# Expert blocks in pairs: 256 moving tokens, gating by chunks, the short rests of two blocks in the row halves of TensorE

## The chip, the cores and the metric

The kernel runs on one core of a Trainium2 chip. The metric is device time in microseconds (us) of one execution; lower is better. All arithmetic is in float32 but for the aggregation of the second layer.

## What is computed

Two layers on 2708 rows of 256 channels, with a 2708 x 2708 adjacency matrix. Each layer is a graph attention step and then a mixture of experts (MoE), each with a residual; layer 0 has an ordinary causal attention ahead of its MoE. Cut to what matters here, the MoE of both layers is:

```python
logits = flat @ router_w.T
topk_probs, topk_idx = top_k(softmax(logits), 2)
gates = ...                      # two of eight experts per row, normalised
for e in range(8):               # w1, w3: 682 x 256, w2: 256 x 682
    hh = silu(flat @ w1[e].T) * (flat @ w3[e].T)
    out = out + gates[:, e:e + 1] * (hh @ w2[e].T)
```

and a layer is

```python
x = x + gnn(layernorm(x), adj)
x = x + ffn(layernorm(x))
```

Layer 1's graph step normalises and projects the rows of layer 0's result (x1 in the kernel), and aggregates them with a masked softmax over the adjacency.

## The kernel before, in words

The rows are cut into 22 tiles of 128. The program runs in four stages: the first layer up to its routing, the experts of layer 0 (experts_blocks with layer 0), the second layer's graph step up to its routing, and the experts of layer 1. A fallback branch at the end is not taken with this input.

**The two list-scheduled stages.** The first and the third stage are lists of steps. Class Plan (L70) holds for each step its engine, an estimated length, what it needs, the buffers that it takes and gives, a rank, and `lands`, the time that is expected to pass from a DMA's issue to its landing. Plan.issue goes through the list with these estimates and writes out the instructions of each engine in the resulting order; so the estimates decide which instruction stands ahead of which in an engine's queue, and the real waits decide when it runs. Gaps that the plan expects on TensorE are filled with matmuls that nobody reads (L1666).

**Places of the experts.** Routing sends each row, by an indirect DMA (L1805), to a place in the buffer xs of the expert that it goes to. Every expert has six blocks of 128 places (NB = 6). Some blocks are not run by experts_blocks but as steps of the lists, by some_blocks: the EARLY ones of layer 0 and of layer 1 (three and four blocks) at the end of the first and third stage, and the two LATE ones of layer 0, (7, 4) and (7, 5), at the head of the third stage. That leaves 43 blocks for experts_blocks in layer 0 and 44 in layer 1. The late blocks are in lines L533 (transposes), L540 (copies on ACT), L555 (up), L561 to L565 (memset and Silu), L570 to L572 (multiplications on DVE), L578 (down), L582 (weighing) and add_rows.

**One block.** The rows of a block are fetched from xs into a tile xt by SP (L2000), transposed on TensorE with the identity (L278) and copied to SBUF by ACT (L280, or L283 with a scale in layer 0): that is front. Then up (L2017) runs 22 matmuls with 128 moving columns: the hidden width of 682 is five chunks of 128 and a rest of 42 (NF = 5, REST = 42), each chunk for w1 and for w3 with two halves of the 256 channels; the rests of w1 and w3 share one weight tile, w3's columns at 0 and w1's at 64 (HIGH). All go to one tile of three PSUM banks, of which there are two. ACT then takes the Silu of all five chunks in one instruction (L2021), DVE multiplies in one (L2022), and both do the rest of 42 rows (L2024, L2025), giving hT. Then down (L2031) runs six matmuls with hT's chunks as weights and 256 columns of w2 as moving data, into y; the sixth chunk is the rest, filled with zeros to 128 rows. DVE weighs y with the gate (L2033), and GpSimd adds the rows to the result in HBM with an indirect accumulating DMA (add_rows, L611). These adds go to the same array, so each waits for the one before it to have landed.

**The order in experts_blocks.** It is written out by hand: in iteration k come the fetch of block k+3, at one place of every expert the load of the weights of expert e+2 into the one of three rooms that e-1 had (load_expert, L1966 to L1978, DMAs on SP, memsets on GpSimd), then up(k), front(k+2), and down(k-1). Tests of the routing's counts on TensorE and DVE stand ahead of block (2, 0). At the end comes the down of the last block.

**The head of the third stage.** x1, the result of layer 0 in HBM, is loaded by SP in five pieces (L1514 to L1517). The first three, up to tile 12, need the adds of experts_blocks to have landed; the last two need the late blocks' adds too. prepare (L1450 on) makes of each tile of x1 the normalised and projected rows: statistics on DVE, a power on GpSimd (L1458), scaling on DVE (L1462), transposes and matmuls on TensorE (L1477), copies on ACT. Masks come from HBM by transposing DMAs (L1541, L1545). Aggregation computes the attention weights (L1556 on ACT, L1565 and L1571 on DVE) and multiplies on TensorE (L1578, into po).

**Memory.** experts_blocks opens pools of its own (bkeep for hT and one room of weights, slot for xt, xT, sl and ys); the third stage's list has its own work tiles. When a pool is closed, the next one takes the same memory, and an instruction that writes there first waits for what last read it.

Of the kernel before, what the change touches and what calls it, by code (L numbers as in the profile page):

```python
# [20 lines left out]
P = 128  # L21
# [124 lines left out]
def adj_ffn_kernel(ctx, tc, x, adj, vecs, bias_rows, tab, w_gnn0, w_gnn1, wqkv, wo,  # L146
# [1263 lines left out]
    def second(X, XB, xs0, x1, x2, sd, mb, xs, arena, load_weights):  # L1410
# [9 lines left out]
        with ExitStack() as s:  # L1420
# [93 lines left out]
            for a, b in zip((0,) + ends, ends):  # L1514
                loads.append(add("SP", 0.45 * (b - a), lambda a=a, b=b: nc.sync.dma_start(
                    out=X[:, a:b, :], in_=x1[a * P:b * P, :].rearrange("(t p) c -> p t c", p=P)),
                    late, rank=-9.0, lands=2.0 if 0 < a < LATE_T else 14.0 if a == 0 else 7.0))  # L1517
                if b == LATE_T:
                    late = some_blocks(add, 0, [(*b, []) for b in LATE], [XR[:, k, :] for k in range(len(LATE))], [],
                                       lambda e: weights_at(arena[:, WE:]), xs0, x1, new, named, -20.0)  # L1520
                    for e in late:
                        e["needs"] += loads
# [289 lines left out]
    def after_all(i, xs):  # L1812
        for name in written[xs.name]:
            tc.add_manual_dep(i.ins, name, NEEDS, reason="reads what they wrote")
# [152 lines left out]
    def load_expert(room, w1, w3, w2, e):  # L1967
        cut = NF * P
        a, b, c, d = weights_at(room)
        nc.gpsimd.memset(c, 0.0)  # L1970
        nc.gpsimd.memset(d[:, NF, :], 0.0)
        w1v, w3v = (w[:, e, :].rearrange("(k p) h -> p k h", p=P) for w in (w1, w3))
        nc.sync.dma_start(out=a, in_=w1v[:, :, :cut])
        nc.sync.dma_start(out=b, in_=w3v[:, :, :cut])
        nc.sync.dma_start(out=c[:, :, :REST], in_=w3v[:, :, cut:])
        nc.sync.dma_start(out=c[:, :, HIGH:], in_=w1v[:, :, cut:])
        nc.sync.dma_start(out=d[:, :NF, :], in_=w2[e, :cut, :].rearrange("(k p) c -> p k c", p=P))
        nc.sync.dma_start(out=d[:REST, NF, :], in_=w2[e, cut:, :])  # L1978

    def experts_blocks(layer, w1, w3, w2, xs, acc, arena):  # L1980

# [3 lines left out]

        with ExitStack() as s:
            keep = s.enter_context(tc.tile_pool(name=f"bkeep{layer}", bufs=1))
            hTs = [keep.tile([P, NHC, P], F32, name=f"hT{i}") for i in range(3)]
            for hT in hTs:
                nc.gpsimd.memset(hT[:, NF, :], 0.0)  # L1990
            rooms = [arena[:, :WE], arena[:, WE:], keep.tile([P, WE], F32, name="room")]

            with tc.tile_pool(name=f"slot{layer}", bufs=2) as sp, \
                    tc.tile_pool(name=f"bpu{layer}", bufs=2, space=PSUM) as pu, \
                    tc.tile_pool(name=f"bpt{layer}", bufs=1, space=PSUM) as pt_:

                def fetch(e, j):
                    xt = sp.tile([P, ROW], F32, tag="xt", name="xt", bufs=5)
                    row = e * CAP + j * P
                    after_all(nc.sync.dma_start(out=xt, in_=xs[row:row + P, :]), xs)  # L2000
                    return xt

                def front(xt):
                    xT = sp.tile([P, KC, P], F32, tag="xT", name="xTs", bufs=3)
                    transpose_row(xT, xt, P, pt_, V_LN2 if layer == 0 else None)
                    return xT

                def up(k, w, xT):

                    pp = pu.tile([P, 3 * GW // P, P], F32, tag="pp", name="pup")  # L2010
                    for n in range(2 * NF + 1):
                        if n < 2 * NF:
                            wn, to = w[n // NF][:, :, n % NF * P:(n % NF + 1) * P], P
                        else:
                            wn, to = w[2], HIGH + REST
                        for c in range(KC):
                            nc.tensor.matmul(pp[:to, n, :], wn[:, c, :], xT[:, c, :],  # L2017
                                             start=(c == 0), stop=(c == KC - 1))
                    hT = hTs[k % len(hTs)]
                    sl = sp.tile([P, NF, P], F32, tag="sl", name="sl")  # L2020
                    nc.scalar.activation(sl, pp[:, :NF, :], AF.Silu)  # L2021
                    nc.vector.tensor_tensor(hT[:, :NF, :], sl, pp[:, NF:2 * NF, :], ALU.mult)  # L2022
                    sr = sp.tile([P, P], F32, tag="sr", name="sr")
                    nc.scalar.activation(sr[:REST], pp[HIGH:HIGH + REST, 2 * NF, :], AF.Silu)  # L2024
                    nc.vector.tensor_tensor(hT[:REST, NF, :], sr[:REST], pp[:REST, 2 * NF, :], ALU.mult)  # L2025
                    return hT

                def down(e, w, hT, xt):
                    y = pt_.tile([P, C], F32, tag="y", name="y")
                    for n in range(NHC):  # L2030
                        nc.tensor.matmul(y, hT[:, n, :], w[3][:, n, :], start=(n == 0), stop=(n == NHC - 1))  # L2031
                    ys = sp.tile([P, C], F32, tag="ys", name="ys", bufs=3)
                    nc.vector.tensor_scalar(ys, y, xt[:, C + 1 + e:C + 2 + e], None, ALU.mult)  # L2033
                    add_rows(layer, acc, ys, xt)

                done = [b[:2] for b in EARLY[layer]] + list(() if layer else LATE)
                blocks = [(e, j) for e in range(NE) for j in range(NB) if (e, j) not in done]
                xt = [fetch(*blocks[k]) for k in range(3)]
                nxt = [front(xt[k]) for k in range(2)]
                last = None  # L2040
                for k, (e, j) in enumerate(blocks):
                    if k + 3 < len(blocks):
                        xt.append(fetch(*blocks[k + 3]))
                    if j == (2 if e else 3) and e + 2 < NE:
                        load_expert(rooms[(e + 2) % 3], w1, w3, w2, e + 2)
                    if (e, j) == (2, 0):

                        pc = pt_.tile([P, C], F32, tag="y", name="pc")
                        nc.tensor.matmul(pc[:, :NE], allones, hsum[:, NT, :], start=True, stop=True)
                        nc.vector.tensor_tensor(counts[:, layer, :], pc[:, :NE], part, ALU.subtract)  # L2050

# [3 lines left out]
                        for i, (e_, t, places, test) in enumerate(tests):  # L2055
# [1 line left out]
                            nc.tensor.matmul(pc[:, at:at + 1], allones, hsum[:, t, e_:e_ + 1], start=True, stop=True)  # L2057
                            to = i + layer * (FLAGS - len(EARLY[1]))
                            nc.vector.tensor_scalar(missed[:, to:to + 1], pc[:, at:at + 1], float(e_ * CAP + places), None, test)
                    if layer == 1 and (e, j) == (3, 0):  # L2060
                        raise_flag(keep, lambda name: pt_.tile([P, C], F32, tag="y", name=name))
                    xT = nxt[k]
                    we = weights_at(rooms[e % 3])
                    hT = up(k, we, xT)
                    if k + 2 < len(blocks):
                        nxt.append(front(xt[k + 2]))
                    if last is not None:
                        down(*last)
# [151 lines left out]
```

## Time and profile before

| | us |
|---|---|
| three runs | 1554.26, 1555.1, 1552.09 (median 1554.26) |
| the profiled execution, whole | 1553.19 |
| its span in the profile | 1551.5 |
| TensorE busy | 1468.3 |
| DVE / ACT / GpSimd busy | 740.9 / 551.9 / 533.0 |
| mean granted TensorE clock | 0.982 of full |

The lines of the profile are read so: a line of a group has the source line, the engine, the operation, output <- inputs, the tile of the PE array that it uses (rows*columns), its shape, how many there are, and after the bar the busy time, the mean in ns of one, and the idle time of the engine just before them with what ended it. A line of the timeline has start, length, engine, source line and operation, how many instructions it sums up, and in brackets the idle time before it and what ended that. SPq is the DMA queue that SP feeds. A float32 matmul shows as two records of the PE. Records overlap in time, because matmuls are pipelined, so what one costs is read from start to start.

The four stages in this execution: the experts of layer 0 run to about 845 us, the second layer's graph step to about 1193 us, the experts of layer 1 from there to the end.

### The profile page before, as it was taken

How to read it: one execution, taken by the hardware profiler on the slowest of the kernel's cores; microseconds unless marked ns; L12 is line 12 of the kernel's file. 1: busy time of each engine (PE TensorE's matmuls, PEld its weight loads, DVE VectorE, ACT ScalarE, POOL GpSimd, SP SyncE). 2: the span in 40 equal slices, each digit the busy share in tenths (PEclk: the TensorE clock that was granted, in tenths of full speed). 3: DMA queues.
4: the chain of work that ended last, by engine and by line, in shares of the span. 5: the costliest groups of instructions: out<-in, count | busy, mean ns of one | idle time of the engine just before them, and what ended most of it. 6: DMA issues, size and time to landing. Idle time of an engine off the chain costs nothing. (4 is left out here: it accounts for less than half of the span.)

```text
span 1551.5 us, 23359 instructions
## 1 busy us (share of the span) xinstructions
PE 1468.3 (95%) x8988; PEld 1153.4 (74%) x8988; DVE 740.9 (48%) x1450; ACT 551.9 (36%) x1068; POOL 533.0 (34%) x695
## 2 busy tenths in 40 slices
PE   6878899999999999999999899999999999999995
PEld 5633433433437899999999678888778999999995
DVE  6688999966685122222221554867753222222221
ACT  3577766754544111111111453443332111111110
POOL 6677679681163222222222300030444222222221
PEclk9899999999999999999999999999999999999998
DMA  7689767620013332333222850541414333332211
GB/s 261 214 274 316 238 231 252 193 67 8 7 54 94 96 75 53 90 90 90 36 36 33 177 117 1 132 111 61 149 58 109 79 87 88 74 87 50 34 34 17
DMA packets 168029, 165.68 MB, mean 107 GB/s; under 512 B 81384, under 2 KB 148264, under 8 KB 165200
## 3 DMA queue, kind: packets, MB, share of 16 engines
q1 hardware_dynamic: 142582, 134.26, 28.5%
q0 software_dynamic: 21056, 26.24, 9.9%
q10 hardware_dynamic: 4270, 3.58, 0.7%
q8 instruction: 73, 1.20, 0.3%
q14 instruction: 48, 0.39, 0.1%
HBM read 87.38 MB, written 61.55 MB: 96 GB/s over the span
## 5 line engine op out<-in xcount | busy, mean ns | idle before, releaser
L2017 PEld LDWEIGHTS pup<-xTs,arena 128*128 128x128 f32 x2772 | 319.2, 191 | 3.7 <-ACT xTs L283 0.7
L2017 PE MATMUL pup<-xTs,arena 128*128 128x128 f32 x2772 | 321.2, 276 | 0.5 <-ACT xTs L283 0.5
L2022 DVE TENSOR_TENSOR hT<-sl,pup 128x640 f32<-128x640 f32 x87 | 71.5, 821 | 451.4 <-ACT sl L2021 451.4
L2021 ACT ACTIVATE sl<-pup 128x640 f32<-128x640 f32 x87 | 61.2, 703 | 504.5 <-PE pup L2017 499.3
L1578 PE MATMUL po<-hb,PT 128*128 128x257 f32 (+2 forms) x968 | 225.9, 388 | 3.7 <-DVE PT L1571 3.7
L1578 PEld LDWEIGHTS po<-hb,PT 128*128 128x128 f32 (+2 forms) x968 | 176.3, 188 | 42.6 <-issue 11.6
L2031 PE MATMUL y<-arena,hT 128*128 128x256 f32 x756 | 173.8, 380 | 0.6 <-DVE ys L2033 0.6
L1100 ACT ACTIVATE e<-stt 128x1024 f32<-128x1024 f32 (+1 forms) x132 | 125.4, 986 | 93.4 <-PE stt L1094 69.0
L1139 DVE TENSOR_TENSOR es<-es,e 128x1024 f32<-128x1024 f32 x104 | 138.0, 1327 | 29.4 <-ACT e L1100 22.9
L2031 PEld LDWEIGHTS y<-arena,hT 128*128 128x128 f32 x756 | 138.8, 190 | 17.2 <-DVE ys L2033 1.0
L611 POOL DMA_INDIRECT out<-ys,xt x44 | 68.3, 1553 | 231.1 <-DVE ys L2033 228.1
L611 POOL DMA_INDIRECT acc<-ys,xt x43 | 67.1, 1560 | 225.8 <-DVE ys L2033 223.9
L1094 PE MATMUL stt<-qT,kT 64*128 64x512 f32 (+1 forms) x528 | 132.9, 614 | 4.6 <-ACT e L1100 4.5
L1805 POOL DMA_INDIRECT xs<-XR,place x88 | 93.7, 1065 | 92.2 <-DVE mk L1565 41.2
L2017 PE MATMUL pup<-xTs,room 128*128 128x128 f32 (+1 forms) x1056 | 123.8, 276 | 0.0
L2017 PEld LDWEIGHTS pup<-xTs,room 128*128 128x128 f32 (+1 forms) x1056 | 121.9, 190 | 1.2
L1120 PE MATMUL o<-e,V 128*64 128x512 f32 (+1 forms) x528 | 122.4, 586 | 0.0
L1556 ACT ACTIVATE E<-sb,dcol 128x768 f32<-128x768 f32 (+1 forms) x88 | 75.1, 858 | 104.4 <-DVE PT L1571 104.0
L1094 PEld LDWEIGHTS stt<-qT,kT 64*128 64x128 f32 x528 | 44.6, 187 | 77.2 <-issue 62.1
L1120 PEld LDWEIGHTS o<-e,V 128*64 128x64 f32 x528 | 32.9, 136 | 68.6 <-issue 52.6
L2033 DVE TENSOR_SCALAR ys<-y,xt 128x256 f32<-128x256 f32 x87 | 42.1, 484 | 54.2 <-PE y L2031 54.2
L2031 PE MATMUL y<-room,hT 128*128 128x256 f32 x288 | 66.1, 379 | 0.0
(275 smaller groups left out, 1922.0 us busy)
## 6 DMA issues: line engine op xcount, KB each, us to landing
arena<-in_adj SPq DMA_DIRECT2D x21, 1354.0 KB, 7.9
arena<-in_w SPq DMA_DIRECT2D x36, 640.0 KB, 4.6
mb<-mb SPq DMA_DIRECT2D x44, 352.0 KB, 2.4
xs<-none SPq DMA_DIRECT2D x16, 804.0 KB, 11.1
xt<-xs SPq DMA_DIRECT2D x87, 134.0 KB, 2.1
room<-in_w SPq DMA_DIRECT2D x12, 640.0 KB, 5.5
acc<-X SPq DMA_DIRECT2D x21, 128.0 KB, 1.7
out<-X SPq DMA_DIRECT2D x21, 128.0 KB, 1.7
```

The costliest lines, as they stand in the source:

```text
L611: nc.gpsimd.indirect_dma_start(out=acc[:, :], out_offset=bass.IndirectOffsetOnAxis(ap=xt[:, C:C + 1].bitcast(I32), axis=0), in_=ys, in_off ...
L1094: nc.tensor.matmul(st[:r, g, c0(sb):], kT[a:b, sb * P:sb * P + r], qT[a:b, t0 + (sb == t0 + 1):t0 + 2, :, :], start=True, stop=True)
L1100: nc.scalar.activation(e[:r, :, c0(sb):], v[sb, "st"][:r, :, c0(sb):], AF.Exp, scale=1.0 / HD ** 0.5)
L1120: nc.tensor.matmul(v["o"][g * HD:(g + 1) * HD, c:], V[:r, sb, g * HD:(g + 1) * HD], v[sb][:r, g, c:], start=(n + i == 0), stop=(n + i == t ...
L1139: nc.vector.tensor_tensor(es, es, v[sb][:r, :, c:], ALU.add)
L1556: nc.scalar.activation(e[:q, :n], sb[:q, i0:i1], AF.Exp, bias=dcol[:q, j:j + 1], scale=SLOPE - 1.0)
L1578: nc.tensor.matmul(v["po", i][:r, :F], v["PT", j][:q, a:a + r], hb[:q, j, :], start=(j == 0), stop=(j == NT - 1))
L1805: i = nc.gpsimd.indirect_dma_start(out=xs[:, :], out_offset=bass.IndirectOffsetOnAxis(ap=at, axis=0), in_=src, in_offset=None)
L2017: nc.tensor.matmul(pp[:to, n, :], wn[:, c, :], xT[:, c, :], start=(c == 0), stop=(c == KC - 1))
L2021: nc.scalar.activation(sl, pp[:, :NF, :], AF.Silu)
L2022: nc.vector.tensor_tensor(hT[:, :NF, :], sl, pp[:, NF:2 * NF, :], ALU.mult)
L2031: nc.tensor.matmul(y, hT[:, n, :], w[3][:, n, :], start=(n == 0), stop=(n == NHC - 1))
```

## The change

The blocks of an expert that experts_blocks runs are taken two at a time, as a unit: layer 0 has 21 pairs and one single block, layer 1 has 21 pairs and two singles.

- fetch loads the one or two blocks of a unit, two units ahead; there are nine xt tiles in place of five.
- front transposes both blocks into one PSUM tile; ACT copies them with one instruction in layer 1 and two in layer 0.
- up runs its 22 matmuls with 256 moving columns, the two blocks side by side. Every chunk has a PSUM bank of its own (five banks in rotation), and is gated by itself: one Silu and one multiplication per chunk of 128 hidden rows and 256 columns. The rest's multiplication is written per block, block 0's into rows 0 to 41 of hT's sixth chunk, block 1's into rows 64 to 105.
- down runs, per block, five matmuls on the full array, and after those of both blocks the two rests, block 0's on rows 0 to 63 and block 1's on rows 64 to 127 of the array. The two y tiles are in two banks. w2's rest is loaded twice by load_expert, to rows 0 and 64. Each block is weighed and added as before; ys has four tiles in place of three.
- load_expert is called at the second unit of an expert (at the first for expert 0).
- In the list of the third stage the `lands` of x1's first three loads are 12.5, 11 and 11 in place of 14, 2 and 2.

The diff:

```diff
--- before.py
+++ after.py
@@ -1514,7 +1514,7 @@
             for a, b in zip((0,) + ends, ends):
                 loads.append(add("SP", 0.45 * (b - a), lambda a=a, b=b: nc.sync.dma_start(
                     out=X[:, a:b, :], in_=x1[a * P:b * P, :].rearrange("(t p) c -> p t c", p=P)),
-                    late, rank=-9.0, lands=2.0 if 0 < a < LATE_T else 14.0 if a == 0 else 7.0))
+                    late, rank=-9.0, lands=12.5 if a == 0 else 11.0 if a < LATE_T else 7.0))
                 if b == LATE_T:
                     late = some_blocks(add, 0, [(*b, []) for b in LATE], [XR[:, k, :] for k in range(len(LATE))], [],
                                        lambda e: weights_at(arena[:, WE:]), xs0, x1, new, named, -20.0)
@@ -1975,7 +1975,9 @@
         nc.sync.dma_start(out=c[:, :, :REST], in_=w3v[:, :, cut:])
         nc.sync.dma_start(out=c[:, :, HIGH:], in_=w1v[:, :, cut:])
         nc.sync.dma_start(out=d[:, :NF, :], in_=w2[e, :cut, :].rearrange("(k p) c -> p k c", p=P))
-        nc.sync.dma_start(out=d[:REST, NF, :], in_=w2[e, cut:, :])
+
+        for q in (0, HIGH):
+            nc.sync.dma_start(out=d[q:q + REST, NF, :], in_=w2[e, cut:, :])
 
     def experts_blocks(layer, w1, w3, w2, xs, acc, arena):
 
@@ -1985,67 +1987,100 @@
 
         with ExitStack() as s:
             keep = s.enter_context(tc.tile_pool(name=f"bkeep{layer}", bufs=1))
-            hTs = [keep.tile([P, NHC, P], F32, name=f"hT{i}") for i in range(3)]
+            hTs = [keep.tile([P, NHC, 2, P], F32, name=f"hT{i}") for i in range(3)]
             for hT in hTs:
-                nc.gpsimd.memset(hT[:, NF, :], 0.0)
+                nc.gpsimd.memset(hT[:, NF, :, :], 0.0)
             rooms = [arena[:, :WE], arena[:, WE:], keep.tile([P, WE], F32, name="room")]
 
             with tc.tile_pool(name=f"slot{layer}", bufs=2) as sp, \
-                    tc.tile_pool(name=f"bpu{layer}", bufs=2, space=PSUM) as pu, \
+                    tc.tile_pool(name=f"bpu{layer}", bufs=5, space=PSUM) as pu, \
                     tc.tile_pool(name=f"bpt{layer}", bufs=1, space=PSUM) as pt_:
 
-                def fetch(e, j):
-                    xt = sp.tile([P, ROW], F32, tag="xt", name="xt", bufs=5)
-                    row = e * CAP + j * P
-                    after_all(nc.sync.dma_start(out=xt, in_=xs[row:row + P, :]), xs)
-                    return xt
-
-                def front(xt):
-                    xT = sp.tile([P, KC, P], F32, tag="xT", name="xTs", bufs=3)
-                    transpose_row(xT, xt, P, pt_, V_LN2 if layer == 0 else None)
+                def bank():
+                    return pt_.tile([P, 2 * C], F32, tag="y", name="y", bufs=2)[:, :C]
+
+                def fetch(unit):
+                    xts = []
+                    for e, j in unit:
+                        xt = sp.tile([P, ROW], F32, tag="xt", name="xt", bufs=9)
+                        row = e * CAP + j * P
+                        after_all(nc.sync.dma_start(out=xt, in_=xs[row:row + P, :]), xs)
+                        xts.append(xt)
+                    return xts
+
+                def front(xts):
+                    B = len(xts)
+                    pt = pt_.tile([P, KC, 2, P], F32, tag="tr", name="pt")
+                    xT = sp.tile([P, KC, 2, P], F32, tag="xT", name="xTs", bufs=3)
+                    for b, xt in enumerate(xts):
+                        for c in range(KC):
+                            nc.tensor.transpose(pt[:, c, b, :], xt[:, c * P:(c + 1) * P], ident)
+                    if layer == 1:
+                        nc.scalar.copy(xT[:, :, :B, :], pt[:, :, :B, :])
+                    else:
+                        for c in range(KC):
+                            nc.scalar.activation(xT[:, c, :B, :], pt[:, c, :B, :], AF.Copy,
+                                                 scale=vec[:, V_LN2 + c:V_LN2 + c + 1])
                     return xT
 
-                def up(k, w, xT):
-
-                    pp = pu.tile([P, 3 * GW // P, P], F32, tag="pp", name="pup")
-                    for n in range(2 * NF + 1):
-                        if n < 2 * NF:
-                            wn, to = w[n // NF][:, :, n % NF * P:(n % NF + 1) * P], P
+                def up(k, w, xT, B):
+
+                    hT = hTs[k % len(hTs)]
+                    for n in range(NHC):
+                        pp = pu.tile([P, 2, 2, P], F32, tag="pp", name="pup")
+                        if n < NF:
+                            parts = [(w[i][:, :, n * P:(n + 1) * P], P) for i in range(2)]
                         else:
-                            wn, to = w[2], HIGH + REST
-                        for c in range(KC):
-                            nc.tensor.matmul(pp[:to, n, :], wn[:, c, :], xT[:, c, :],
-                                             start=(c == 0), stop=(c == KC - 1))
-                    hT = hTs[k % len(hTs)]
-                    sl = sp.tile([P, NF, P], F32, tag="sl", name="sl")
-                    nc.scalar.activation(sl, pp[:, :NF, :], AF.Silu)
-                    nc.vector.tensor_tensor(hT[:, :NF, :], sl, pp[:, NF:2 * NF, :], ALU.mult)
-                    sr = sp.tile([P, P], F32, tag="sr", name="sr")
-                    nc.scalar.activation(sr[:REST], pp[HIGH:HIGH + REST, 2 * NF, :], AF.Silu)
-                    nc.vector.tensor_tensor(hT[:REST, NF, :], sr[:REST], pp[:REST, 2 * NF, :], ALU.mult)
+                            parts = [(w[2], HIGH + REST)]
+                        for i, (wn, to) in enumerate(parts):
+                            for c in range(KC):
+                                nc.tensor.matmul(pp[:to, i, :B, :], wn[:, c, :], xT[:, c, :B, :],
+                                                 start=(c == 0), stop=(c == KC - 1))
+                        sl = sp.tile([P, 2, P], F32, tag="sl", name="sl", bufs=3)
+                        if n < NF:
+                            nc.scalar.activation(sl[:, :B, :], pp[:, 0, :B, :], AF.Silu)
+                            nc.vector.tensor_tensor(hT[:, n, :B, :], sl[:, :B, :], pp[:, 1, :B, :], ALU.mult)
+                        else:
+                            nc.scalar.activation(sl[:REST, :B, :], pp[HIGH:HIGH + REST, 0, :B, :], AF.Silu)
+                            for b in range(B):
+                                q = HIGH * b
+                                nc.vector.tensor_tensor(hT[q:q + REST, n, b, :], sl[:REST, b, :],
+                                                        pp[:REST, 0, b, :], ALU.mult)
                     return hT
 
-                def down(e, w, hT, xt):
-                    y = pt_.tile([P, C], F32, tag="y", name="y")
-                    for n in range(NHC):
-                        nc.tensor.matmul(y, hT[:, n, :], w[3][:, n, :], start=(n == 0), stop=(n == NHC - 1))
-                    ys = sp.tile([P, C], F32, tag="ys", name="ys", bufs=3)
-                    nc.vector.tensor_scalar(ys, y, xt[:, C + 1 + e:C + 2 + e], None, ALU.mult)
-                    add_rows(layer, acc, ys, xt)
+                def down(e, w, hT, xts):
+
+                    ys = [bank() for _ in xts]
+                    for b, y in enumerate(ys):
+                        for n in range(NF):
+                            nc.tensor.matmul(y, hT[:, n, b, :], w[3][:, n, :], start=(n == 0), stop=False)
+                    for b, y in enumerate(ys):
+                        part_ = slice(HIGH * b, HIGH * (b + 1)) if len(ys) > 1 else slice(0, P)
+                        nc.tensor.matmul(y, hT[part_, NF, b, :], w[3][part_, NF, :], start=False, stop=True)
+                    for y, xt in zip(ys, xts):
+                        yw = sp.tile([P, C], F32, tag="ys", name="ys", bufs=4)
+                        nc.vector.tensor_scalar(yw, y, xt[:, C + 1 + e:C + 2 + e], None, ALU.mult)
+                        add_rows(layer, acc, yw, xt)
 
                 done = [b[:2] for b in EARLY[layer]] + list(() if layer else LATE)
-                blocks = [(e, j) for e in range(NE) for j in range(NB) if (e, j) not in done]
-                xt = [fetch(*blocks[k]) for k in range(3)]
-                nxt = [front(xt[k]) for k in range(2)]
-                last = None
-                for k, (e, j) in enumerate(blocks):
-                    if k + 3 < len(blocks):
-                        xt.append(fetch(*blocks[k + 3]))
-                    if j == (2 if e else 3) and e + 2 < NE:
-                        load_expert(rooms[(e + 2) % 3], w1, w3, w2, e + 2)
-                    if (e, j) == (2, 0):
-
-                        pc = pt_.tile([P, C], F32, tag="y", name="pc")
+                units = []
+                for e in range(NE):
+                    left = [(e, j) for j in range(NB) if (e, j) not in done]
+                    units += [left[i:i + 2] for i in range(0, len(left), 2)]
+                xt = [fetch(u) for u in units[:2]]
+                nxt = [front(x) for x in xt[:2]]
+                last, asked = None, 1
+                for k, unit in enumerate(units):
+                    e = unit[0][0]
+                    if k + 2 < len(units):
+                        xt.append(fetch(units[k + 2]))
+
+                    if e + 2 < NE and asked < e + 2 and (k == 0 or units[k - 1][0][0] == e):
+                        asked = e + 2
+                        load_expert(rooms[asked % 3], w1, w3, w2, asked)
+                    if unit[0] == (2, 0):
+
+                        pc = bank()
                         nc.tensor.matmul(pc[:, :NE], allones, hsum[:, NT, :], start=True, stop=True)
                         nc.vector.tensor_tensor(counts[:, layer, :], pc[:, :NE], part, ALU.subtract)
 
@@ -2057,12 +2092,11 @@
                             nc.tensor.matmul(pc[:, at:at + 1], allones, hsum[:, t, e_:e_ + 1], start=True, stop=True)
                             to = i + layer * (FLAGS - len(EARLY[1]))
                             nc.vector.tensor_scalar(missed[:, to:to + 1], pc[:, at:at + 1], float(e_ * CAP + places), None, test)
-                    if layer == 1 and (e, j) == (3, 0):
-                        raise_flag(keep, lambda name: pt_.tile([P, C], F32, tag="y", name=name))
-                    xT = nxt[k]
+                    if layer == 1 and unit[0] == (3, 0):
+                        raise_flag(keep, lambda name: bank())
                     we = weights_at(rooms[e % 3])
-                    hT = up(k, we, xT)
-                    if k + 2 < len(blocks):
+                    hT = up(k, we, nxt[k], len(unit))
+                    if k + 2 < len(units):
                         nxt.append(front(xt[k + 2]))
                     if last is not None:
                         down(*last)
```

## The prediction, made before the changed kernel was run

> **What bounds the kernel now.** I read the head of the page first, then the groups by line, then the timeline at four places: a steady stretch of expert blocks, and the three seams around them (blocks of layer 0 to second layer, second layer to blocks of layer 1, the end).
>
> ```profile
> span 1551.5 us, 23359 instructions
> PE 1468.3 (95%) x8988; PEld 1153.4 (74%) x8988; DVE 740.9 (48%) x1450; ACT 551.9 (36%) x1068; POOL 533.0 (34%) x695
> ...
> PE   6878899999999999999999899999999999999995
> ...
> L2031 PE MATMUL y<-arena,hT 128*128 128x256 f32 x756 | 173.8, 380 | 0.6 <-DVE ys L2033 0.6
> ...
> L1094 PE MATMUL stt<-qT,kT 64*128 64x512 f32 (+1 forms) x528 | 132.9, 614 | 4.6 <-ACT e L1100 4.5
> ```
>
> TensorE is busy 95% of the span, and before the expert matmuls it idles 0.6 us in all: only TensorE's own time counts inside the blocks. One block in the steady stretch, timeline of TensorE:
>
> ```profile
> 700.14 0.38 PE L278 MATMUL pt<-ident,xt 128*128 128x128 f32 x2
> 700.36 2.76 PE L2031 MATMUL y<-arena,hT 128*128 128x256 f32 x12
> 702.95 5.06 PE L2017 MATMUL pup<-xTs,arena 128*128 128x128 f32 x44
> 707.85 0.38 PE L278 MATMUL pt<-ident,xt 128*128 128x128 f32 x2
> ```
>
> Starts give 0.22 us of transposes, 2.59 for 12 records of y (216 ns each, 256 columns), 4.90 for 44 records of up (111.4 ns each, 128 columns): 7.71 us per block. A float32 matmul is two records. The page's mean ns of one (380) is latency, so I price by starts.
>
> The seams are chains, not throughput. Layer 0's end, then layer 1's start:
>
> ```profile
> 842.28 1.55 POOL L611 DMA_INDIRECT acc<-ys,xt  x1 [5.93 <-DVE ys L2033]
> ...
> 846.79 1.57 POOL L611 DMA_INDIRECT acc<-ys,xt  x1 [1.44 <-DMA acc<-ys,xt]
> ...
> 847.38 8.78 PE L555 MATMUL up<-xTs,arena 128*128 128x128 f32 x76 [0.24 <-ACT xTs L540]
> ...
> 850.64 1.45 SPq L1515 DMA_DIRECT2D X<-acc  x3
> ```
>
> ```profile
> 1187.39 2.26 SPq L2000 DMA_DIRECT2D xt<-xs  x5
> ...
> 1193.37 1.57 POOL L611 DMA_INDIRECT out<-ys,XR  x1 [4.28 <-DVE ys L582]
> ...
> 1194.36 5.07 PE L2017 MATMUL pup<-xTs,arena 128*128 128x128 f32 x44
> ```
>
> An add (L611) starts only when the one before has landed: 842.28 to 846.79 is 4.51 us, and landing follows issue by 3.85 (846.79 to 850.64). x1's loads wait for the last landing while the late blocks keep TensorE busy. Layer 1's first fetches do not wait for the early blocks' adds.
>
> **What the Trainium skill says.** "TensorE: Matmul & The Clock Gate", "Wait — 56ns, not 53.3ns?": a warm matmul costs its columns plus a fixed 2.5 ns or so. The trace agrees in kind: twice 111.4 against 216 leaves 6.8 ns per record; I use that. Same page, "What's actually happening": an idle window of about 3.4 us halves the clock. The trace has it: after 4.88 us of idle at 861, the stretch 861.0 to 864.5 shows clock 0.51. "TensorEngine Tiling (Array Packing)", "Key Properties": row tiles work independently, and changing the mode drains TensorE. The trace agrees: L1094's two row halves start 6 ns apart and a pair takes 427 ns for 512 columns; a change from whole array to row halves costs 95 ns beyond the work, back 92. "DMA: Bandwidth & Descriptors", "Rules for kernel authors": accumulating DMAs on the same bytes must wait for each other, which is the 4.51 us above.
>
> **Part by part.**
> Up, transposes, full down. Per pair: 44 records of 256 columns × 0.216 = 9.51 (before 2 × 4.90 = 9.80), transposes 0.44 as before, 20 records of y × 0.216 = 4.32 as before. Gain 0.29.
> Rests in row halves. Before 4 records × 0.216 = 0.864. After, two pairs of halves side by side, 2 × 0.216, plus the two mode changes 0.187: 0.619. Gain 0.245. Bounds: −0.43 (changes free) to +0.19 (halves not side by side).
> A pair: 14.89 against 15.42, −0.53. There are 42 pairs and 3 singles (87 blocks): **−22.4**.
> Gating by chunk. From 640 elements 703 ns and 128 elements 273 (ACT), 822 and 278 (DVE), 256 elements give about 380 and 415. Per pair ACT has 6 of these and the copy, 3.1 us; DVE 7 and two weighings, 3.8. Both are under a quarter of 14.9 and hidden by the 1.73 us that TensorE spends on a chunk with five PSUM banks; without that cover a chunk would cost some 1.1 us. Nothing.
> Fetches and adds. A unit's two fetches ride SP two units ahead; with 9 xt buffers the second waits for an add of four blocks back, landing about 7 to 8 us into the unit, and is needed at 9.5. POOL's two adds take 9 of 14.9. Slack 1 to 2 us, price of failing in a rival. Behind a late fetch on SP stands only the weight load, needed a unit later. The extra w2 load (43 KB, 12 times) is hidden by DMA at a 0.25 share there. Nothing. Two fetches before the first block and POOL's count tests: **+0.7**.
> Seam of layer 0. Call T1 the end of y of the last unit but one. Before, two adds remain, and the last lands at T1 + 9.2 (841.47 to 850.64). After, the last two units are pairs, four adds remain: 0.25 + 4 × 4.55 = T1 + 18.45. Of the 9.25, 2.35 is the extra down after T1, already in the sum: the landing comes 6.9 later. The built program shows also that the late blocks' first copy (L540) and so its up (L555), POOL's memset (L561) and a DVE cast now wait for that last landing, since the larger block pools lie under the second stage's work tiles; behind them on ACT, POOL and DVE queues stands the rest of the list. So the late block no longer covers the wait: it starts 0.5 after the landing instead of 3.3 before (+3.8), on half clock after some 12 us of idle (+1.7). Back come the 4.88 us of idle at 861: with the new landing times the list puts the late block's multiplications (L570) ahead of x1's statistics on DVE (−4.9), and about 2 of preparation are done earlier, next late being the prepared rows. 6.9 + 3.8 + 1.7 − 4.9 − 2: **+5.5**, bounds +2 (aggregation waits for masks anyway) and +12 (nothing recovered, two half-clock windows). The list change itself moves no DMA past another on SP; only the order on DVE, ACT and PE.
> Layer 1's start. The built program shows the first fetch on SP, and so transposes and up behind it, waiting for the last early add, whose memory the larger pools take. It is issued at 1193.37 and lands 3.85 later, 1197.2; fetch 2.3, transposes and copy 1.7: up at 1201.2 instead of 1194.36, +6.8, and half clock for part of a window, 1.6: **+8.4**, bounds +6 and +10.5 (two windows).
> The end. Before, the last add lands two steps after T1; after, four: 9.1 later, less 2.35 counted: **+6.7**, bounds 5.5 and 7.5.
> Sum: −22.4 + 0.7 + 5.5 + 8.4 + 6.7 = −1.1 against the profiled 1553.19, so 1552.1. That execution is 1.07 below the median of the runs, 1554.26: forecast 1553.2.
>
> **Rivals.**
> 1. The seams are cheaper: +2, +6, +5.5. For: aggregation also waits for masks and DMA is at a 0.77 share there, so later x1 may be hidden. Against: the first aggregation follows x1's load by 45 us with PE idle in between. −22.4 + 0.7 + 13.5 = −8.2: 1546.
> 2. Slower: the seam of layer 0. With late blocks and x1 released by one landing, both want DVE and ACT at once. Price 12 there, and 10.5 at layer 1's start if that clock stays low: −22.4 + 0.7 + 12 + 10.5 + 6.7 = +7.5, 1561.8. It decides from +9.7 at the first seam on, the others as forecast. For: half clock follows each such idle in the trace. Against: the idle at 861 is recoverable.
> 3. Row halves don't run side by side in accumulation: rests 0.864 + 0.187, a pair 15.32: −4.3 in place of −22.4, 1571. Against: L1094 and L1120 do run so.
> 4. Late fetches: half a microsecond on each of some 40 units is +20, 1573. Against: the slack above.
>
> **How the numbers follow.** Forecast case 40% (own range 1549 to 1558), rival 1 27%, rival 2 23%, rivals 3 and 4 together 10%. 0.2% (3.1 us) is about what a measurement of this kernel can tell from no change. Faster than 1551.1: most of rival 1 and a quarter of the forecast case, 34%; slower than 1557.4: most of rival 2, rivals 3 and 4, 33%; within, 33%. Range 1543 to 1564: outside lie a little of rivals 1 and 2, and rivals 3 and 4, some 20% in all.
>
> **What would show it.** In the changed profile: a pair's period of 14.9 us (15.3 would be rival 3, above 15.5 with TensorE idle before transposes rival 4); rest records in row halves starting a few ns apart; after layer 0's last y, TensorE idle some 12 us until an add lands, then clock near 0.5; L570 ahead of x1's statistics; layer 1's first fetch after the last early add lands; four adds 4.5 us apart at the end. I am wrong if TensorE keeps working through either seam (too dear), or if the first aggregation comes more than 10 us later against T1 (too cheap).

## The result and the profile after

The changed kernel takes 1558.28 us, median of six runs (1553.35 to 1559.81); the kernel before, in six runs beside it, 1552.92 (1552.09 to 1555.1). The ratio is 1.0032, 95% interval 1.002 to 1.0044: slower by about 5 us. The profiled execution took 1557.49 (span 1555.5), against 1553.19 (1551.5) before. The two traces differ by 4.1 us in span, close to what the runs show, so they can be compared piece by piece.

The head of the page, after:

```profile
span 1555.5 us, 19869 instructions
PE 1449.8 (93%) x7118; PEld 1058.9 (68%) x7118; DVE 758.9 (49%) x1588; ACT 565.7 (36%) x1101; POOL 532.8 (34%) x695
...
PE   6878999999999999999997899999998999999994
```

TensorE is busy for 18.5 us less, and the span is longer: idle time has come in. The steady stretch of layer 0's experts, timeline of TensorE:

```profile
697.45 9.76 PE L2037 MATMUL pup<-xTs,arena 128*128 128x256 f32 x44
707.05 0.60 PE L2017 MATMUL pt<-ident,xt 128*128 128x128 f32 x4
707.48 4.48 PE L2056 MATMUL y<-arena,hT 128*128 128x256 f32 x20
711.90 0.70 PE L2059 MATMUL y<-arena,hT 64*128 64x256 f32 x4
712.53 9.76 PE L2037 MATMUL pup<-xTs,room 128*128 128x256 f32 x44
```

From start to start (712.53 less 697.45) a pair takes 15.08 us, where 14.89 was forecast and two blocks took 15.42 before. No idle time shows in it: gating, fetches and adds are hidden as forecast. The end of layer 0's blocks, all engines:

```profile
837.67 1.56 POOL L611 DMA_INDIRECT acc<-ys,xt  x1 [2.94 <-issue]
...
842.29 1.57 POOL L611 DMA_INDIRECT acc<-ys,xt  x1 [2.74 <-issue]
846.74 1.56 POOL L611 DMA_INDIRECT acc<-ys,xt  x1 [2.88 <-issue]
...
850.60 2.28 SPq L1515 DMA_DIRECT2D X<-acc  x3
851.18 1.14 ACT L540 ACTIVATE xTs<-pt,vec 128x128 f32<-128x128 f32 x4 [23.33 <-DVE identb L1430]
...
851.60 10.91 PE L555 MATMUL up<-xTs,arena 128*128 128x128 f32 x76 [9.25 <-ACT xTs L540]
...
857.71 0.69 DVE L570 TENSOR_TENSOR chunks<-chunks,up 128x512 f32<-128x512 f32 x1 [6.85 <-PE up L555]
```

The adds follow each other at 4.5 us; x1's load and the late block's copy on ACT start within 0.6 us of each other, both on the last landing, and TensorE has idled 9.25 us by then. L570 then stands ahead of x1's statistics. The start of layer 1's experts:

```profile
1189.43 1.57 POOL L611 DMA_INDIRECT out<-ys,XR  x1 [3.13 <-DVE ys L582]
1193.29 4.14 SPq L2007 DMA_DIRECT2D xt<-xs  x9
...
1195.41 1.44 PE L2017 MATMUL pt<-ident,xt 128*128 128x128 f32 x4 [6.79 <-DMA xt<-xs]
...
1198.13 11.04 PE L2037 MATMUL pup<-xTs,arena 128*128 128x256 f32 x44
```

The first fetch follows the last early block's add by 3.86 us, which is its landing. The first up lasts 11.04 in place of 9.76: the trace has the granted clock at 0.50 of full for 10.24 us from 1190.7 on, which ends at 1200.9, within this up. The end:

```profile
1528.68 1.55 POOL L611 DMA_INDIRECT out<-ys,xt  x1 [8.60 <-DVE ys L2062]
...
1533.20 1.55 POOL L611 DMA_INDIRECT out<-ys,xt  x1 [2.97 <-issue]
...
1538.45 1.55 POOL L611 DMA_INDIRECT out<-ys,xt  x1 [3.70 <-DVEq L2201]
1542.97 1.55 POOL L611 DMA_INDIRECT out<-ys,xt  x1 [2.97 <-issue]
```

When the last weighing ends, at 1534.6, the second of four adds is under way; for the last 21 us only the adds run, and what closes the program.

The span, cut at the same events in both traces (us; after each layer's last up there is now a pair's down twice instead of a block's, 4.8 us more by the trace, and this is put with the pairs):

| piece | before to after | forecast |
|---|---|---|
| experts of layer 0 and 1, by pairs | -14.4 | -22.4 and +0.7 |
| layer 0's last landing | +6.7 | +6.9 |
| from there to layer 1's last early add | -3.9 | -1.4 |
| layer 1's start, with its half clock | +9.0 | +8.4 |
| the end | +6.6 | +6.7 |
| sum, before rounding | +4.1 | -1.1 |

### The profile page after: what moved, and what is told of

Same layout as the page of the kernel before. It is cut to its first block, busy times and chain, and to the rows that moved or that the text cites. A ratio compares the mean times of both kernels' runs of the same rounds, so it can differ in the third digit from the quotient of the medians.

```text
span 1555.5 us, 19869 instructions
## 1 busy us (share of the span) xinstructions
PE 1449.8 (93%) x7118; PEld 1058.9 (68%) x7118; DVE 758.9 (49%) x1588; ACT 565.7 (36%) x1101; POOL 532.8 (34%) x695
## 5 line engine op out<-in xcount | busy, mean ns | idle before, releaser
L2037 PE MATMUL pup<-xTs,arena 128*128 128x256 f32 (+3 forms) x1452 | 312.3, 375 | 0.6 <-ACT xTs L2022 0.6
L2037 PEld LDWEIGHTS pup<-xTs,arena 128*128 128x128 f32 (+1 forms) x1452 | 263.8, 190 | 45.0 <-issue 8.9
L2041 ACT ACTIVATE sl<-pup 128x256 f32<-128x256 f32 (+1 forms) x225 | 84.8, 377 | 486.9 <-PE pup L2037 484.8
L2042 DVE TENSOR_TENSOR hT<-sl,pup 128x256 f32<-128x256 f32 (+1 forms) x225 | 92.8, 413 | 306.1 <-ACT sl L2041 304.4
L1578 PE MATMUL po<-hb,PT 128*128 128x257 f32 (+2 forms) x968 | 224.3, 386 | 0.8 <-DVE PT L1571 0.7
L1578 PEld LDWEIGHTS po<-hb,PT 128*128 128x128 f32 (+2 forms) x968 | 175.0, 187 | 39.4 <-issue 12.2
L2056 PE MATMUL y<-arena,hT 128*128 128x256 f32 x630 | 141.6, 379 | 1.1 <-DVE ys L2062 1.1
L1094 PE MATMUL stt<-qT,kT 64*128 64x512 f32 (+1 forms) x528 | 131.9, 610 | 5.8 <-ACT e L1100 5.4
L2062 DVE TENSOR_SCALAR ys<-y,xt 128x256 f32<-128x256 f32 x87 | 38.2, 480 | 191.0 <-PE y L2059 191.0
L2056 PEld LDWEIGHTS y<-arena,hT 128*128 128x128 f32 x630 | 117.4, 190 | 16.8 <-DVE ys L2062 1.9
L1120 PE MATMUL o<-e,V 128*64 128x512 f32 (+1 forms) x528 | 122.4, 586 | 0.0
L2037 PE MATMUL pup<-xTs,room 128*128 128x256 f32 (+1 forms) x528 | 119.3, 383 | 0.0
L2037 PEld LDWEIGHTS pup<-xTs,room 128*128 128x128 f32 (+1 forms) x528 | 97.8, 188 | 16.9 <-issue 3.6
L1094 PEld LDWEIGHTS stt<-qT,kT 64*128 64x128 f32 x528 | 44.5, 187 | 78.0 <-issue 63.2
L1120 PEld LDWEIGHTS o<-e,V 128*64 128x64 f32 x528 | 32.9, 136 | 68.6 <-issue 53.5
L968 DVE MAX8 tops<-arena 128x8 f32<-128x2708 f32 (+1 forms) x22 | 65.3, 2969 | 1.0 <-DMA arena<-in_adj 1.0
```

The source lines that it names most:

```text
L1094: nc.tensor.matmul(st[:r, g, c0(sb):], kT[a:b, sb * P:sb * P + r], qT[a:b, t0 + (sb == t0 + 1):t0 + 2, :, :], start=True, stop=True)
L1120: nc.tensor.matmul(v["o"][g * HD:(g + 1) * HD, c:], V[:r, sb, g * HD:(g + 1) * HD], v[sb][:r, g, c:], start=(n + i == 0), stop=(n + i == t ...
L1578: nc.tensor.matmul(v["po", i][:r, :F], v["PT", j][:q, a:a + r], hb[:q, j, :], start=(j == 0), stop=(j == NT - 1))
L2037: nc.tensor.matmul(pp[:to, i, :B, :], wn[:, c, :], xT[:, c, :B, :], start=(c == 0), stop=(c == KC - 1))
L2041: nc.scalar.activation(sl[:, :B, :], pp[:, 0, :B, :], AF.Silu)
L2042: nc.vector.tensor_tensor(hT[:, n, :B, :], sl[:, :B, :], pp[:, 1, :B, :], ALU.mult)
```

## The experiments

The kernel before ran beside each group of experiments, and its median lay between 1552.3 and 1557.6 in the different groups. So sizes here come from ratios to it, times 1552.9. "Give or take" is the 95% half-interval of a difference between two kernels: the root of the sum of the squares of their two half-intervals.

**Rests on the whole array.** What the forecast priced at 0.245 us a pair, undone.

```diff
-    part_ = slice(HIGH * b, HIGH * (b + 1)) if len(ys) > 1 else slice(0, P)
+    part_ = slice(0, P)
...
-    q = HIGH * b
+    q = 0
...
-        for q in (0, HIGH):
-            nc.sync.dma_start(out=d[q:q + REST, NF, :], in_=w2[e, cut:, :])
+        nc.sync.dma_start(out=d[:REST, NF, :], in_=w2[e, cut:, :])
```

> The changed kernel with both rests as matmuls on the whole array (rows 0 to 127, zeros below row 42), no row halves and w2's rest loaded once. Theory (a change of tile shape costs twice: 93 to 97 ns of drain, and 104 ns more on the first records after it, so 0.39 us for the two changes of a pair): a pair becomes 4 x 0.216 = 0.864 for the rests against 2 x 0.216 + 0.394 = 0.826, so +0.04 us x 42 = +1.6 us against the changed kernel, about the same time. Rival (the forecast's price of 0.19 for the two changes, and the loss is elsewhere in the pair): +0.245 x 42 = +10 us.

Measured: ratio 1.0053 (1.0033 to 1.0074), so +3.3 us against the changed kernel, give or take 3.7. The runs exclude the rival's +10, but cannot tell +1.6 from nothing; the length of one pair in the trace can. Its timeline of TensorE:

```profile
699.17 9.66 PE L2036 MATMUL pup<-xTs,arena 128*128 128x256 f32 x44
708.66 0.60 PE L2016 MATMUL pt<-ident,xt 128*128 128x128 f32 x4
709.10 4.48 PE L2055 MATMUL y<-arena,hT 128*128 128x256 f32 x20
713.42 1.03 PE L2058 MATMUL y<-arena,hT 128*128 128x256 f32 x4
714.28 9.66 PE L2036 MATMUL pup<-xTs,room 128*128 128x256 f32 x44
```

15.11 us from start to start: the row halves were worth 0.03 us a pair, not 0.245. Up is 9.49 here (708.66 less 699.17) and 9.60 in the changed kernel, though its 44 records are the same: 0.1 us is lost at its start, behind the halves.

**Four changes of shape in a pair.** The suspected cost doubled: each block's rest directly behind its five full matmuls.

```diff
     for b, y in enumerate(ys):
         for n in range(NF):
             nc.tensor.matmul(y, hT[:, n, b, :], w[3][:, n, :], start=(n == 0), stop=False)
-    for b, y in enumerate(ys):
         part_ = slice(HIGH * b, HIGH * (b + 1)) if len(ys) > 1 else slice(0, P)
```

> The changed kernel with each block's rest directly after its five full matmuls, so four changes of tile shape in a pair instead of two and no halves side by side. Theory (0.197 us a change): 4 x 0.216 + 4 x 0.197 = 1.652 against 0.826, +0.83 us a pair, +35 us in all. Rival (0.094 a change, the 104 ns being something of the place, not of the change): 0.864 + 4 x 0.094 + 0.208 = 1.448, +0.62 a pair, +26 us.

Measured in a single execution: 1586.38 us. Its pair, timeline of TensorE:

```profile
703.62 9.76 PE L2037 MATMUL pup<-xTs,arena 128*128 128x256 f32 x44
713.22 0.60 PE L2017 MATMUL pt<-ident,xt 128*128 128x128 f32 x4
713.66 2.32 PE L2056 MATMUL y<-arena,hT 128*128 128x256 f32 x10
715.91 0.70 PE L2058 MATMUL y<-arena,hT 64*128 64x256 f32 x2
716.54 2.43 PE L2056 MATMUL y<-arena,hT 128*128 128x256 f32 x10
718.90 0.70 PE L2058 MATMUL y<-arena,hT 64*128 64x256 f32 x2
719.52 8.68 PE L2037 MATMUL pup<-xTs,room 128*128 128x256 f32 x39
```

15.90 us, +0.82 against the changed kernel: the theory's 0.83, not the rival's 0.62. The span grew by 28.9 us rather than 35: counted from the last up, layer 0's last add comes 2.4 us earlier than in the changed kernel and the end of the program 2.8, presumably because a pair's adds are spread out more.

**The block tiles' pool ahead of hT and the weights' room.**

```diff
+            sp = s.enter_context(tc.tile_pool(name=f"slot{layer}", bufs=2))
             keep = s.enter_context(tc.tile_pool(name=f"bkeep{layer}", bufs=1))
...
-            with tc.tile_pool(name=f"slot{layer}", bufs=2) as sp, \
-                    tc.tile_pool(name=f"bpu{layer}", bufs=5, space=PSUM) as pu, \
+            with tc.tile_pool(name=f"bpu{layer}", bufs=5, space=PSUM) as pu, \
```

> The changed kernel with only the order of two pools exchanged (block tiles ahead of hT and the third room of weights), so that neither the late blocks of layer 0 nor the first fetches of layer 1 write where the last adds still read. Theory (memory that is reused too early makes the seams wait): the first up of layer 1 comes 1 us after the last early add in place of 8.7 and at full clock, -9 us; at layer 0's end the late block runs before the landing as in the kernel before, -1 to -4 more: -9 to -13 us against the changed kernel. Rival (another wait takes its place: the two-block fetch, half clock): -3 us at most.

Measured: ratio 0.9948 (0.9933 to 0.9963), so 13 us less than the changed kernel, give or take 3. The timeline at both places:

```profile
842.94 1.57 POOL L611 DMA_INDIRECT acc<-ys,xt  x1 [2.69 <-issue]
842.99 1.15 ACT L540 ACTIVATE xTs<-pt,vec 128x128 f32<-128x128 f32 x4 [14.37 <-PE pt L533]
...
851.79 1.45 SPq L1515 DMA_DIRECT2D X<-acc  x3
```

```profile
1184.91 4.19 SPq L2007 DMA_DIRECT2D xt<-xs  x9
...
1190.47 1.57 POOL L611 DMA_INDIRECT out<-ys,XR  x1 [4.28 <-DVE ys L582]
...
1191.99 4.27 PE L2037 MATMUL pup<-xTs,arena 128*128 128x256 f32 x19
```

The late block's copy starts 8.8 us ahead of x1's load, the first fetch 5.6 ahead of the last early add, and up 1.5 behind that add. The waits were those for memory that is used again, as the order of the pools alone removes them. Nothing took their place.

**Single blocks at the ends.**

```diff
+                single = units[-2:]
+                units[-2:] = [[b] for u in single for b in u]
```

> The changed kernel with the last two pairs of each layer run as four single blocks. Theory (adds land one after another, 4.5 us apart, and a pair leaves four of them for the end instead of two): the end of layer 1 is 6.8 us shorter, that of layer 0 too, of which the seam gives on all or half, and four lost pairs cost 4 x 0.34 = 1.4: -9 us, bounds -5 and -12. Rival (what follows layer 0's blocks waits for something else, and the end is set by the last down): -1 us.

Measured: ratio 0.9951 (0.9932 to 0.997): 12.6 us less than the changed kernel, give or take 3.5, at the far bound of the theory. In its trace the last piece, from the last up on, is 20.9 us in place of 33.0; x1's load is issued at 844.18 instead of 850.60.

```profile
1527.62 1.55 POOL L611 DMA_INDIRECT out<-ys,xt  x1 [5.95 <-DVE ys L2062]
...
1529.45 0.48 DVE L2062 TENSOR_SCALAR ys<-y,xt 128x256 f32<-128x256 f32 x1 [2.10 <-PE y L2059]
1532.14 1.55 POOL L611 DMA_INDIRECT out<-ys,xt  x1 [2.96 <-issue]
```

Only one add is left queued behind the last weighing.

**The landing times alone, in three settings.** First, taken out of the changed kernel:

```diff
-                    late, rank=-9.0, lands=12.5 if a == 0 else 11.0 if a < LATE_T else 7.0))
+                    late, rank=-9.0, lands=2.0 if 0 < a < LATE_T else 14.0 if a == 0 else 7.0))
```

> The changed kernel with the landing times of x1's loads as before (14, 2 and 2). Theory (the order on DVE decides: with the old times x1's statistics stand ahead of the late block's multiplications and TensorE waits for these): +3 to +6 us against the changed kernel. Rival (both are released by the same landing, and the order doesn't matter): within 1 us.

Measured: ratio 1.0044 (1.0029 to 1.006), +1.9 us, give or take 3.0: by the runs it is open between the two. Two lines of the trace, of DVE and of TensorE, speak for the rival:

```profile
857.50 0.69 DVE L570 TENSOR_TENSOR chunks<-chunks,up 128x512 f32<-128x512 f32 x1
858.24 2.86 PE L578 MATMUL pt<-arena,chunks 128*128 128x256 f32 x12
```

x1's statistics stand ahead of L570 again, but up starts only with the landing that releases x1 too (at 847.97, 1.0 behind x1's load), and runs until L578 follows it without idle: the 4.9 us are not there. Then put into the kernel before, with the reverse edit:

> The kernel before with nothing but the new landing times. If the order on DVE is worth its 4.9 us of idle: -3 to -5 us against the kernel before. If aggregation then waits elsewhere: within 1 us.

Measured: ratio 0.9937 (0.9921 to 0.9953): 9.8 us less than the kernel before, twice what was expected. This line of the kernel before shows the idle time in question:

```profile
861.04 4.54 PE L578 MATMUL pt<-arena,chunks 128*128 128x256 f32 x12 [4.88 <-DVE chunks L570]
```

With the new times the 4.88 us at L578 are 0.81. The profiled execution (1550.09) was the slowest of its six, and its aggregation ran 17.1 us at half clock against 9.6 in the profile of before; so how the other 5 us divide stays open.

**Both seams repaired**, by the pools' order and the single ends together:

> The changed kernel with both repairs: the block tiles' pool ahead of hT and the third room, and the last two pairs of each layer as single blocks. Theory (the two costs lie in different places and add, and what is left of the change is the 0.34 us per pair): -13 and -10, less some 3 that both gave back at layer 0's end: about -20 us against the changed kernel, -14 (0.9%) against the kernel before. Rival (both shorten the same wait): -13 us against the changed kernel.

Measured: ratio 0.9855 (0.9836 to 0.9873), 27.5 us less than the changed kernel, give or take 3.4. The two savings (13.0 and 12.6) add: they are different waits. Against the kernel before it is 22.5 us faster. And with the old landing times in it:

> As the run with both repairs, with the landing times of before. Here the late block runs before the landing again, so the order on DVE can matter again as it did in the kernel before. Theory (new times help only because x1 lands late): within 2 us of the run with both repairs. Rival (the new order is worth the 4.9 us of idle of the kernel before by itself): +3 to +5 us against it.

Measured: ratio 0.9975 (0.9965 to 0.9986), 18.6 us more than with the new ones, far beyond the theory and beyond the rival. TensorE's timeline of this kernel after layer 0:

```profile
859.73 4.54 PE L578 MATMUL pt<-arena,chunks 128*128 128x256 f32 x12 [4.77 <-DVE chunks L570]
...
877.03 0.44 PE L1468 MATMUL pt<-ident,xn 128*128 128x128 f32 x2 [1.86 <-DVE xn L1462]
...
895.35 1.23 PE L1578 MATMUL po<-hb,PT 128*128 128x257 f32 x2 [4.08 <-DVE PT L1571]
```

Of these three idles, 10.7 us in all, the new times leave 1.21 ahead of L1468 and 0.81 ahead of L1578. Cut at the same events, the two traces differ by 5.9 us from x1's load to the first aggregation, and by 10.4 from there to layer 1's last early add. On this whole way TensorE ran 23.9 us at half clock here and 10.2 with the new times, worth half of the difference, 6.9, most of it in the second part; some 4 us of the second part are not explained. So the theory that new times help only because x1 lands late falls: it is the other way round. In these three pairs of kernels they help where the late block runs ahead of the landing (9.8 and 18.6 us), and hardly where it is held up by it, as in the changed kernel (1.9).

**Rests of two units together**, on both repairs: half as many changes of shape.

```diff
...
+                    group.append((e, w, hT, xts, ys))
+                    if last or len(group) == 2 or len(xts) == 1:
+                        rests()
...
```

> The kernel with both seams repaired, and the rests of two units run together where two pairs follow each other (16 groups of four halves, two changes of shape each, where 32 pairs had two each); y has four PSUM banks, up three, xt fourteen tiles. Theory (0.394 us for each way out and back): -16 x 0.394 = -6.3 us against the kernel with both seams repaired, a period of two pairs of 29.77 instead of 30.16. Rival (four adds at once and three banks for up make new waits that eat it): no gain, idle time of TensorE before up or before the transposes.

Measured: ratio 0.9833 (0.9818 to 0.9848), 3.4 us less than with both repairs alone, give or take 3.7: by the runs not to be told from no change. Two pairs, timeline of TensorE:

```profile
669.68 9.76 PE L2037 MATMUL pup<-xTs,arena 128*128 128x256 f32 x44
...
698.38 1.14 PE L2066 MATMUL y<-arena,hT 64*128 64x256 f32 x8
699.45 9.76 PE L2037 MATMUL pup<-xTs,arena 128*128 128x256 f32 x44
```

29.77 us, to the hundredth what the theory says. Of the 6.3 us of the theory the two stages of experts show 3.8 in the traces: a wait of 1.27 us for a gated chunk at the start of layer 1 and three stops of 0.3 us where the rests run early, ahead of the count tests, take most of the rest.

**Both repairs, rests on the whole array.**

> The kernel with both seams repaired and the rests on the whole array as in the kernel before. Theory (the row halves gain 0.04 us a pair): +1.5 us against the kernel with both seams repaired, not to be told from no change. Rival (forecast's price): +9 us.

Measured: ratio 0.9849 (0.983 to 0.9868), 0.9 us less than with the halves, give or take 4.1: no difference, as the theory says; +9 is excluded.

## Why the prediction was wrong

**The step that failed is "Rests in row halves".** It put the two mode changes at 0.187 us, 95 and 92 ns beyond the work, and the gain at 0.245 a pair. That is only the wait ahead of the first record of the new shape. The first record (or pair of halves) after a change then also takes 104 ns more until the next can start. The changed kernel's trace shows it record by record:

```profile
711.59 0.38 PE L2056 MATMUL y<-arena,hT 128*128 128x256 f32 x1
711.90 0.49 PE L2059 MATMUL y<-arena,hT 64*128 64x256 f32 x2
712.22 0.38 PE L2059 MATMUL y<-arena,hT 64*128 64x256 f32 x2
712.53 0.48 PE L2037 MATMUL pup<-xTs,room 128*128 128x256 f32 x1
712.85 0.38 PE L2037 MATMUL pup<-xTs,room 128*128 128x256 f32 x1
```

To the nanosecond these starts lie 309, 320, 313 and 320 ns apart, where 216 would be the work. So the two changes cost 93 + 104 + 97 + 104 = 398 ns, and the rests 0.83 us against 0.864. By this term a pair came out 0.19 us longer than forecast (15.08 for 14.89), over 42 pairs 8.0 us: the experts gave 14.4 where 22.4 was forecast, and of the +0.7 put at their starts next to nothing shows. This alone turns the forecast -1.1 into +6.9. That it is the change of shape, and not its place, follows from the runs with no change (15.11 us a pair), two (15.08), four (15.90) and two for every two pairs (29.77): each fits 0.197 us a change to 0.02 us or better. Why the first record is slow stays open.

The trace of before had the second half: the first pair of L1094 at 311.22 runs 533 ns to the next, the ones after it 428. I had read the starts across the change and not the one after it. The Trainium skill, "TensorEngine Tiling (Array Packing)", "Key Properties", says that a mode change drains TensorE. It gives no time for it; here 93 to 97 ns of wait stand ahead of the new shape, and the 104 ns behind come on top.

**Up with 256 columns** was right: 9.49 without a change of shape ahead of it, against 9.51 forecast.

**Layer 0's seam** was right in its first part: the landing came 6.7 later, and the late block waited for it and began at half clock. In all the seam cost 2.8, not 5.5, but that is luck in the main. From x1's load to the first aggregation the trace shows +0.5, with 16 matmul records of preparation more in it than before (the "2 of preparation done earlier" of the forecast, 2.6 us by their starts). The aggregation stage is 4.4 shorter: 3.1 because 9.6 us at half clock became 3.4 there, and the other 1.3 is less than what that preparation took. Nothing in the forecast speaks of this clock, and nothing shows that it belongs to the change: the run with four changes of shape, with the same code in this stage, has 10.2 us at half clock in it. Without the 3.1 the seam would be at 5.9, beside 5.5. The landing times as such saved about 2 in this place, by the run without them and within its uncertainty, less than the 4.9 that I counted; these belong to the case in which the late block runs first.

**Layer 1's start** (+9.0 for +8.4) and **the end** (+6.6 for +6.7) were right, mechanism and size; the run with the pools' order and the one with single ends show each cause. That nothing inside the blocks becomes late was right too.

**The rivals.** It ended on the slower side, but not by rival 2, whose first seam at 12 measured 2.8. Rival 3 was wrong as told (halves start 6 to 7 ns apart) and right in effect: the halves gain next to nothing, 0.03 us a pair. The range, 1543 to 1564, held 1558.28; the forecast of no change, at 1553.2, did not hold beside +0.32%.

**What the change was worth by parts**: against the kernel before, the new landing times alone -9.8 us; pairs on top of them with both seams repaired -12.7 (0.9855 against 0.9937); the seams, as the change leaves them, +27.5. These parts depend on the order in which they are taken: without the new times, pairs with both seams repaired are worth only -3.9 (0.9975), and the times then -18.6. The kernel with both repairs, with the rests in halves, on the whole array or grouped, runs at 0.9855, 0.9849 and 0.9833 of the kernel before, and the runs do not tell these three apart.

## What to carry to other kernels

A change of TensorE's tile shape is priced at the wait before the first record and at that record's own delay, so read the starts on both sides of it. In this kernel's case (from the whole array to row halves, float32, 256 columns) small tiles must save more than 0.4 us for each way out and back. Work made coarser in a loop is paid at its ends: count what is left in a serial chain when the last unit is done, and look at which buffers of the next stage lie on memory that this chain still reads. An order written by estimates is worth what waits behind it: its gain changes when a release moves.

## What the runs showed that was not expected

The 104 ns are not the tile shape's alone: in the kernel before, the first record of L1195 after 2.17 us of idle (308.29) also takes 320 ns to the next where 216 is usual. Nor are they the same for every shape: the first pair of L1120, in tiles of 128*64, takes 479 ns at 309.35 where the next take 430.

The stretches of half clock weigh on what a seam costs beyond its wait: from x1's load to layer 1's last early add they add up to between 10.2 and 23.9 us in the traces, which moves this way by up to 7 us. The forecast tied half clock to idle time ahead of it, but not every stretch has any. In the changed kernel's trace the clock is 0.50 from 1033.7 to 1037.1, and TensorE was busy there all the time:

```profile
1023.79 14.38 PE L1578 MATMUL po<-hb,PT 128*128 128x257 f32 x56
```

What starts such a stretch is not shown here.
